# Products of attention values in 64x64 tiles of TensorE, for both sequences of a head group at once

## The chip, the cores and the metric

The kernel runs on one core of a Trainium2 chip. The metric is the device time of one execution in microseconds. Before the change it is 921.83 us, the median of three runs (920.75 to 923.23).

## The reference, cut to what matters

Sixteen sequences of 256 tokens of width 256 pass through two layers, each of the form x + s(xn) * silu(f(xn)) with xn the layer norm of x. In the first layer s is a linear recurrence and f a feed-forward block. In the second, s is causal attention with 16 heads and a key-value latent of 64, and f a linear layer with routed low-rank experts. Only the attention is touched:

```python
kv = x @ Wkv_a
c_kv, k_rope = (kv[..., :KV_LORA], kv[..., KV_LORA:])
c_kv = c_kv * rsqrt(mean(c_kv * c_kv) + RMS_EPS) * kv_norm_w
kv = (c_kv @ Wkv_b).reshape(B, S, N_HEADS, QK_NOPE + V_DIM)
scores = jnp.where(mask, einsum('bqhd,bkhd->bhqk', q, k) * scale, min)
attn = softmax(scores)
out = einsum('bhqk,bkhd->bqhd', attn, v).reshape(B, S, N_HEADS * V_DIM)
return out @ Wo
```

The kernel folds Wkv_b into the query weights and into Wo. So scores are taken against the 128 values of a key row (64 latent, 64 rotated), and the product of values multiplies the probabilities with the 64 latent values c_kv alone.

## The kernel before

All data are float32. The first 300 us are the first layer; behind it comes a loop (line 1603) over 64 units. A chunk is 512 tokens, that is two sequences (b = 0 and 1); its 16 heads form four groups g of G = 4 heads. A unit is one sequence of one group, so a group is two successive units and a chunk eight (r = 0 to 7). Helpers at the top record every operation in the order of the program for each engine (class InOrder); therefore nearly every instruction of the profile has line 53, and the reading goes by tile names.

For a unit, score_pack (line 1354) makes the scores in three packs, each in one PSUM bank of a ring of three (tile sc): block a of 32 queries of four heads stands in 128 partitions and meets the 32 (a + 1) keys that the causal mask leaves. VectorE (DVE) masks the diagonal and takes the maxima (nm); ScalarE (ACT) writes the exponentials to pr and their sums to sr; normalise (line 1386) takes reciprocals on DVE and scales pr on GpSimd (POOL).

The product needs the probabilities with keys in partitions. turn (line 1399) transposes 32x32 squares on DVE into the tile turned, in three thirds: queries 0 to 127 with keys 0 to 127, queries 128 to 255 with keys 0 to 127, and queries 128 to 255 with keys 128 to 255. send (line 1411) writes turned to DRAM (tile far, three buffers) with four DMAs, one for each head, and fetch (line 1423) brings it back as pT with one DMA, so that 128 keys stand in partitions; pT has three buffers. values (line 1442) then multiplies, for each pair of heads p2, each key block kb of 128 and each head hh of the pair: the stationary operand is the 64 latent values of 128 key rows (k.row), the moving operand pT, 256 columns for the first block and 128 for the second, and the output 64 partitions (half hh) of a PSUM bank av. ACT copies av to attT, which finish_mm or fast_mm multiply with the output weights. For the last two units turn_here (line 1427) transposes on PE instead of going through DRAM.

The order in the loop is written by hand. In unit i, SP first gets fetch of unit i - 2, later send of unit i - 1, and in even units query_move (line 419), eight DMAs that place rotated queries into qg. PE takes values of units i - 4 and i - 3 together in even i, between score packs 1 and 2 (units 0 and 1 at i = 4 and 5, the last ones behind the loop). All DMAs of SP stand in one queue and are issued one by one; an issue that waits holds those behind it.

The latent rows come about once per chunk: kv_begin (line 266) at r = 4 and kv_end (line 293) at r = 5 write k.row of the next chunk, with two buffers; key_chunk (line 299) at r = 7 transposes it to kT for the scores. The working tiles of PE's results (m1: av, pq and others) share a ring of five PSUM banks.

Of the kernel before, what the change touches and what calls it, by code (L numbers as in the profile page):

```python
# [11 lines left out]
F32 = mybir.dt.float32  # L12
# [6 lines left out]
P = 128  # L19
B, S, D = 16, 256, 256  # L20
NTOK = B * S
CH = 512
NCH = NTOK // CH
TPC = CH // P
# [5 lines left out]
NOPE, ROPE, VD, KVL = 128, 64, 128, 64  # L30
# [11 lines left out]
def tile_two_layers(ctx: ExitStack, tc: tile.TileContext, d: dict, out: bass.AP):  # L42
# [54 lines left out]
    pe = InOrder(nc.tensor)  # L97
# [103 lines left out]
    def bc(ap, n):  # L201

        return ap.unsqueeze(1).to_broadcast([ap.shape[0], n, ap.shape[1]])
# [8 lines left out]
    ak = ctx.enter_context(tc.tile_pool(name="ak1", bufs=2))  # L212
# [5 lines left out]
    sp = InOrder(nc.sync)  # L218
    ve = InOrder(nc.vector)
    ac = InOrder(nc.scalar)  # L220
# [3 lines left out]
    def m1(name, shape):  # L224
        return place["pool"].tile(shape, F32, tag=place["tag"], name=name)
# [4 lines left out]
    chunks = [Chunk() for _ in range(NCH)]  # L230
# [35 lines left out]
    def kv_begin(ch):  # L266

        k = chunks[ch]
        k.pkv = pkv = m1(f"pkv_{ch}", [P, TPC, P])
        for j in range(TPC):  # L270
            for c in range(2):
                pe.matmul(
                    pkv[:, j, :], k.xnT[:, c, j * P : (j + 1) * P], wkva[:, c, :],
                    start=(c == 0), stop=(c == 1),
                )
        k.row = ak.tile([P, TPC, P], F32, tag="row", name=f"row_{ch}")
        k.tmp = tmp = ak.tile([P, 3, TPC, KVL], F32, tag="tmp", name=f"tmp_{ch}", bufs=1)
        sq, ra, rb = tmp[:, 0], tmp[:, 1], tmp[:, 2]
        ss = sm1.tile([P, TPC], F32, tag="ss", name=f"ss_{ch}")
        k.rk = sm1.tile([P, TPC], F32, tag="rk", name=f"rk_{ch}")  # L280
        ac.activation(sq, pkv[:, :, 0:KVL], AF.Square)
        x1_ = pkv[:, :, KVL : KVL + HR]
        x2_ = pkv[:, :, KVL + HR : P]
        ve.tensor_tensor(ra[:, :, 0:HR], x1_, rope_k[:, 0], ALU.mult)
        ve.tensor_tensor(ra[:, :, HR:ROPE], x2_, rope_k[:, 0], ALU.mult)
        ve.tensor_tensor(rb[:, :, 0:HR], x2_, rope_k[:, 1], ALU.mult)
        ve.tensor_tensor(rb[:, :, HR:ROPE], x1_, rope_k[:, 2], ALU.mult)
        ve.tensor_reduce(ss, sq, AX.X, ALU.add)
        ve.tensor_scalar(ss, ss, 1.0 / KVL, RMS_EPS, ALU.mult, ALU.add)
        gp.tensor_tensor(k.rk, ss, mhalf, ALU.pow)  # L290
        gp.tensor_tensor(k.row[:, :, KVL:P], ra, rb, ALU.add)

    def kv_end(ch):
        k = chunks[ch]
        sq = k.tmp[:, 0]
        ve.tensor_tensor(sq, k.pkv[:, :, 0:KVL], bc_in(k.rk, KVL), ALU.mult)
        ve.tensor_tensor(k.row[:, :, 0:KVL], sq, bc(kvw_bc, TPC), ALU.mult)

    def key_chunk(ch):
        k = chunks[ch]  # L300
# [67 lines left out]
    G = 4  # L368
    NG = NH // G
# [59 lines left out]
    with ExitStack() as l0:  # L429
# [151 lines left out]
        u = tiny("u")  # L581
# [234 lines left out]
        def fast_weights1():  # L816
            w12 = x1.tile([P, 2, FH], F32, tag="xnT", name="w12")
            w56 = x1.tile([P, 2, FH], F32, tag="xn", name="w56", bufs=1)
            fw.w = {1: w12[:, 0], 2: w12[:, 1], 5: w56[:, 0], 6: w56[:, 1]}
            fw.w[7] = ak.tile([P, FH], F32, tag="kT", name="w7")  # L820
            g = g0
            g.tensor_tensor(fw.w[1], a1(0, 0), a1(1, 1), ALU.add)
            g.tensor_tensor(fw.w[5], a1(0, 0), a1(0, 1), ALU.add)
            g.tensor_tensor(fw.w[2], a1(1, 0), a1(1, 1), ALU.add)
            g.tensor_tensor(fw.w[6], a1(0, 0), a1(1, 0), ALU.subtract)
            g.tensor_tensor(fw.w[7], a1(1, 1), a1(0, 1), ALU.subtract)
            fw.w[3], fw.w[4] = a1(0, 0), a1(1, 1)
            x36 = ak.tile([P, 2, S], F32, tag="row", name="x36")
            x417 = ak.tile([P, 3, S], F32, tag="tmp", name="x417", bufs=1)
            fw.x = {3: x36[:, 0], 4: x417[:, 0], 1: x417[:, 1]}  # L830
            fw.x6 = [x36[:, 1], w0.tile([P, S], F32, tag="bst", name="x6")]
            fw.x7 = [x417[:, 2], w0.tile([P, S], F32, tag="bsc", name="x7")]
            misc = qr.tile([P, 2, CH], F32, tag="qrot", name="misc")
            fw.f = misc[:, 0, :].rearrange("p (i s) -> p i s", i=2)
            fw.db = misc[:, 1, 0:DH]

        def fast_weights2():
            t12 = x1.tile([P, 2, 4, DH], F32, tag="xnT", name="t12")
            fw.t = {1: t12[:, 0], 2: t12[:, 1]}
            fw.t[3] = ak.tile([P, 4, DH], F32, tag="row", name="t3")  # L840
            fw.t[4] = ak.tile([P, 4, DH], F32, tag="kT", name="t4")
            g = g0
            g.tensor_tensor(fw.t[1], b2(0, 1), b2(0, 0), ALU.subtract)
            g.tensor_tensor(fw.t[2], b2(1, 1), fw.t[1], ALU.subtract)
            g.tensor_tensor(fw.t[4], fw.t[2], b2(1, 0), ALU.subtract)
            g.tensor_tensor(fw.t[3], b2(1, 1), b2(0, 1), ALU.subtract)
            g.tensor_tensor(fw.db, b2_bc[:, DH:D], b2_bc[:, 0:DH], ALU.subtract)
# [562 lines left out]

    def send(u):

        u.far = dp.tile([4, 32, G, 3, P], F32, tag="far", name=f"far_{u.n}", bufs=3)
        for h in range(G):
            sp.dma_start(
                u.far[:, :, h, :, :].rearrange("k s z q -> s k z q"),
                u.turned[32 * h : 32 * h + 32, :, :, :],
            )

    def new_pT(u):  # L1420
        u.pT = pp.tile([P, G, 3, P], F32, tag="pT", name=f"pT_{u.n}", bufs=3)

    def fetch(u):
        new_pT(u)
        sp.dma_start(u.pT, u.far.rearrange("k s h z q -> (k s) h z q"))

    def turn_here(u, z):

        if z == 1:
            new_pT(u)  # L1430
        a0, k0 = THIRDS[z]
        pt = m1(f"pt_{u.n}_{z}", [P, CH])
        for y in range(4):
            o = OFF[a0] + y * WID[a0] + 32 * k0
            pe.transpose(pt[:, y * P : (y + 1) * P], u.pr[:, o : o + P], ident)
        for y, e in ((0, ac.copy), (2, ve.tensor_copy)):
            e(
                u.pT[:, :, z, 32 * y : 32 * y + 64].rearrange("p h (a q) -> p a h q", q=32),
                pt[:, y * P : (y + 2) * P].rearrange("p (a h q) -> p a h q", a=2, h=G),
            )  # L1440

    def values(u, e=None):
        k, b = chunks[u.ch], u.b
        av = m1(f"av_{u.n}", [P, 2, S])
        for p2 in range(2):
            for kb in range(2):
                for hh in range(2):
                    h = 2 * p2 + hh
                    pe.matmul(
                        av[64 * hh : 64 * hh + 64, p2, P * kb : S].rearrange(  # L1450
                            "p (z s) -> p z s", s=P
                        ),
                        k.row[:, 2 * b + kb, 0:KVL],
                        u.pT[:, h, 2:3, :] if kb else u.pT[:, h, 0:2, :],
                        start=(kb == 0), stop=(kb == 1),
                    )
        if b == 0:
            k.attT.append(a2.tile([P, 2, CH], F32, tag="attT", name=f"attT_{u.n}", bufs=6))
        (e or ac.copy)(k.attT[u.g][:, :, b * S : (b + 1) * S], av)

    def finish_mm(ch, j, p0, p1):
        k = chunks[ch]
        if p0 == 0:
            if ch == NCH - 1 and j < 3:
                k.po[j] = ps_sc.tile([P, CH], F32, tag="sc", name=f"po_{ch}_{j}")
            else:
                k.po[j] = m1(f"po_{ch}_{j}", [P, CH])
        for p in range(p0, p1):
            pe.matmul(
                k.po[j][:, 0:D], k.attT[p // 2][:, p % 2, j * P : (j + 1) * P], wout[:, p, :],  # L1470
                start=(p == 0), stop=(p == NPAIR - 1),
            )
# [130 lines left out]
    for i in range(LAST):  # L1603
# [7 lines left out]
        last = ch - 1 if ch == NCH - 1 and r in FINISH else None  # L1611
        fast = ch - 1 if 0 < ch < NCH - 1 else None

        if 2 <= i:
            fetch(units[i - 2])
        score_pack(u, 0)
        if w:
            normalise(w, (2,))
# [28 lines left out]
            if not odd:  # L1647
                query_lat(n, 3)
        if i == 5:
            values(units[1])  # L1650
        score_pack(u, 1)

        if odd and n is not None:
# [10 lines left out]
        if not odd:  # L1664
            if n is not None and i != 2:
                query_move(n)
            if i >= 4:
                values(units[i - 4])
            if i > 4:
                values(units[i - 3])  # L1670
        score_pack(u, 2)
        normalise(u, (0, 1))

# [25 lines left out]
    normalise(u1, (2,))  # L1699

    finish_mm(ch, 0, 0, 4)
    values(units[LAST - 4])
    finish_mm(ch, 1, 0, 4)
    turn_here(u1, 1)
    turn_here(u1, 2)
    values(units[LAST - 3], ve.tensor_copy)
    values(u0)
    turn_here(u1, 0)
    for j in range(TPC):
# [80 lines left out]
```

## Time and profile before

| what | value |
|---|---|
| median of the runs | 921.83 us |
| span of the profiled execution | 919.9 us, 1.9 less than that median |
| mean granted TensorE clock | 0.996 |
| PE, DVE, POOL, ACT busy | 905.2, 666.4, 570.6, 465.8 us |
| fetches pT<-far | 62 of 768 KB, 5.0 us from issue to landing |
| sends far<-turned | 248 of 192 KB, 4.3 us |
| moves qg<-qrot | 256 of 64 KB, 2.3 us |

The span runs from the first to the last instruction of one execution; what lies around it (start and end) is in the time and not in the span. "Busy" is time in which an engine has at least one instruction, so that two products which run at once count once; the mean duration of one record stands behind it. PEld is the loading of stationary operands, which runs beside the products. "a<-b" names the tile that is written and a tile that is read. The chain of work that ended last follows the execution back from its end, at each step to what released it; what is not on it did not set the end.

### The profile page before, as it was taken

How to read it: one execution, taken by the hardware profiler on the slowest of the kernel's cores; microseconds unless marked ns; L12 is line 12 of the kernel's file. 1: busy time of each engine (PE TensorE's matmuls, PEld its weight loads, DVE VectorE, ACT ScalarE, POOL GpSimd, SP SyncE). 2: the span in 40 equal slices, each digit the busy share in tenths (PEclk: the TensorE clock that was granted, in tenths of full speed). 3: DMA queues.
4: the chain of work that ended last, by engine and by line, in shares of the span. 5: the costliest groups of instructions: out<-in, count | busy, mean ns of one | idle time of the engine just before them, and what ended most of it. 6: DMA issues, size and time to landing. Idle time of an engine off the chain costs nothing.

```text
span 919.9 us, 17382 instructions
## 1 busy us (share of the span) xinstructions
PE 905.2 (98%) x5426; PEld 695.4 (76%) x5426; DVE 666.4 (72%) x2018; ACT 465.8 (51%) x1529; POOL 570.6 (62%) x885
## 2 busy tenths in 40 slices
PE   8999999999999899999999999999999999999998
PEld 7768898987767567777777777777777777777776
DVE  6876687664688779668967866896786689677562
ACT  3335555654336545645644564564466456446541
POOL 1228697777355537686586767648676764866541
PEclk9999999999999999999999999999999999999999
DMA  9730000000025777777776777777677777767771
GB/s 280 232 115 1 1 2 1 1 2 1 1 32 106 201 203 184 203 186 186 178 210 160 208 194 192 189 178 207 159 209 206 181 190 178 205 160 211 206 224 42
DMA packets 196412, 134.00 MB, mean 146 GB/s; under 512 B 142112, under 2 KB 186976, under 8 KB 196320
## 3 DMA queue, kind: packets, MB, share of 16 engines
q1 hardware_dynamic: 194192, 128.68, 53.3%
q0 software_dynamic: 1152, 3.67, 1.2%
q8 instruction: 44, 0.72, 0.3%
q10 hardware_dynamic: 976, 0.53, 0.2%
q14 instruction: 48, 0.39, 0.1%
HBM read 63.11 MB, written 52.95 MB: 126 GB/s over the span
## 4 chain that ended last, share of the span: by engine, by line
PE 90%; DVE 3%; DMA 2%; SPq 2%; POOL 1%; issue 1%; ACT 0%; POOLq 0%; DVEq 0%; ACTq 0%
PE pq L53 22%; PE sc L53 14%; PE po L53 10%; PE av L53 9%; PE r L53 7%; PE f L53 7%; PE ph L53 5%; PE pf L53 5%; PE pg L53 4%; PE pm L53 2%; SPq L53 2%; PE pkv L53 1%; PE tp L53 1%; DMA qg<-qrot 1%; PE py L53 1%; PE pb L53 1%
## 5 line engine op out<-in xcount | busy, mean ns | idle before, releaser
L53 ACT ACTIVATE pr<-sc,nm 128x256 f32<-128x256 f32 (+7 forms) x512 | 189.7, 381 | 240.3 <-DVE sr L53 152.2
L53 POOL TENSOR_SCALAR pr<-pr,sr 128x256 f32<-128x256 f32 (+7 forms) x512 | 192.1, 394 | 190.0 <-DVE sr L53 184.1
L53 PEld LDWEIGHTS sc<-kT,qg 128*128 128x128 f32 x1024 | 157.6, 191 | 62.3 <-issue 40.3
L53 PE MATMUL sc<-kT,qg 128*128 128x256 f32 (+7 forms) x1024 | 176.1, 306 | 5.7 <-DMA qg<-qrot 4.4
L53 DVE TENSOR_REDUCE nm<-sc 128x1 f32<-128x256 f32 (+7 forms) x512 | 127.5, 301 | 6.6
L53 DVE STREAM_TRANSPOSE turned<-pr 128x512 f32<-128x512 f32 x186 | 123.2, 687 | 9.6 <-POOL pr L53 8.7
L53 PE MATMUL pq<-xnT,wlat 128*128 128x512 f32 x256 | 124.1, 608 | 0.0
L53 PE MATMUL pq<-xnT,wrope 128*128 128x512 f32 x256 | 120.2, 593 | 0.0
L53 ACT ACTIVATION_READ_ACCUMULATOR pr<-sc,nm 128x1 f32 x512 | 104.3, 204 | 0.0
L53 DVE TENSOR_TENSOR sc<-sc,kmask 128x96 f32<-128x96 f32 (+1 forms) x192 | 45.5, 237 | 64.9 <-PE sc L53 63.9
L53 PE MATMUL av<-pT,row 128*64 128x256 f32 (+1 forms) x1024 | 90.9, 329 | 0.5 <-DMA pT<-far 0.5
L53 POOL TENSOR_TENSOR qrot<-qmul,qmul 128x512 f32<-128x512 f32 x64 | 83.0, 1317 | 8.0 <-POOL pr L53 2.9
L53 PEld LDWEIGHTS av<-pT,row 128*64 128x64 f32 x1024 | 64.1, 137 | 24.3 <-issue 1.6
L53 DVE TENSOR_TENSOR qmul<-pq,rot_q 128x512 f32<-128x512 f32 x128 | 80.7, 672 | 0.1
L53 ACT ACTIVATE qg<-pq 64x512 f32<-64x512 f32 x128 | 75.4, 589 | 5.4 <-PE pq L53 4.7
L53 PEld LDWEIGHTS pq<-xnT,wlat 128*128 128x128 f32 x256 | 46.0, 192 | 32.0 <-issue 32.0
L53 PEld LDWEIGHTS pq<-xnT,wrope 128*128 128x128 f32 x256 | 45.7, 191 | 32.4 <-issue 32.1
L53 PEld LDWEIGHTS po<-wout,attT 128*128 128x128 f32 x416 | 58.4, 191 | 9.5 <-issue 4.9
L53 PE MATMUL po<-wout,attT 128*128 128x128 f32 (+1 forms) x416 | 64.5, 308 | 0.0
L53 POOL TENSOR_TENSOR rs<-ve,mhalf 128x4 f32<-128x4 f32 (+1 forms) x17 | 16.8, 986 | 51.3 <-DVE ve L53 37.0
L53 PE MATMUL ph<-xnT,p1T 128*128 128x256 f32 (+1 forms) x128 | 44.3, 503 | 0.8 <-DVE xnT L53 0.8
L53 POOL TENSOR_TENSOR attT<-attT,attT 128x512 f32<-128x512 f32 x36 | 45.0, 1270 | 0.0
(226 smaller groups left out, 1505.0 us busy)
## 6 DMA issues: line engine op xcount, KB each, us to landing
far<-turned SPq DMA_DIRECT2D x248, 192.0 KB, 4.3
pT<-far SPq DMA_DIRECT2D x62, 768.0 KB, 5.0
qg<-qrot SPq DMA_DIRECT2D x256, 64.0 KB, 2.3
x<-in_x_dram SPq DMA_DIRECT2D x7, 512.0 KB, 9.3
out_dram<-x POOLq DMA_DIRECT2D x12, 256.0 KB, 4.9
wqn_wo<-in_wq_nopeT_dram SPq DMA_DIRECT2D x4, 512.0 KB, 4.9
wqn_wo<-in_Wo_dram SPq DMA_DIRECT2D x4, 512.0 KB, 6.1
p2T<-in_proj2T_dram SPq DMA_DIRECT2D x2, 512.0 KB, 7.2
```

What stands on the lines that cost most here:

```text
L53: r = getattr(self.engine, name)(*args, **kw)
```

## The change

The products of values of a group are made for both sequences together (values_of), with keys in blocks of 64. Partitions 0 to 63 of the operands hold sequence 0 and partitions 64 to 127 sequence 1; an output half hh and a sequence b together name one 64x64 tile of TensorE, and av has one PSUM bank for each sequence. The moving operand is that of two heads at once, with 512, 384, 256 and 128 columns for key blocks 0 to 3. The stationary operand comes from a new tile rowv, in which kv_end places the latent rows with four copies on ACT; k.row now has one buffer. far holds a whole group (two buffers), and fetch brings it in odd units with four DMAs of 64 partitions into one pT with a single buffer. values_of(n) stands in unit i = 2n + 4 (group 0 at i = 5); group 30 is behind the loop, and the last group is made as before, with its pT in the buffers of turned.

```diff
 def kv_end(ch):
...
+        if ch == 0:
+            rowv.append(ak.tile([P, 2, 4, KVL], F32, tag="rowv", name="rowv", bufs=1))
+        k.rowv = rowv[0][:, ch % 2]
+        for b in range(2):
+            for y in range(2):
+                ac.copy(
+                    k.rowv[64 * b : 64 * b + 64, y::2, :],
+                    k.row[64 * y : 64 * y + 64, 2 * b : 2 * b + 2, 0:KVL],
+                )
...
-        u.far = dp.tile([4, 32, G, 3, P], F32, tag="far", name=f"far_{u.n}", bufs=3)
+        q = groups[u.i // 2]
+        if u.b == 0:
+            q.far = dp.tile([2, 4, 32, G, 3, P], F32, tag="far", name=f"far_{u.n}", bufs=2)
...
-    def fetch(u):
-        new_pT(u)
-        sp.dma_start(u.pT, u.far.rearrange("k s h z q -> (k s) h z q"))
+    def fetch(n):
+
+        q = groups[n]
+        q.pT = pp.tile([P, 2, G, 3 * P], F32, tag="pT", name=f"pT_{n}", bufs=1)
+        far = q.far.rearrange("b (y k) s h z q -> y b (k s) (h z q)", y=2)
+        for y in range(2):
+            for b in range(2):
+                sp.dma_start(
+                    q.pT[64 * b : 64 * b + 64, y].rearrange("p h q -> p (h q)"), far[y, b]
+                )
...
+    def values_of(n):
+
+        q = groups[n]
+        ch, g = divmod(n, NG)
+        k = chunks[ch]
+        av = [m1(f"av_{ch}_{g}_{b}", [P, 2, S]) for b in range(2)]
+        for z, c0 in enumerate((0, 64, S, S + 64)):
+            n0 = 64 * z
+            heads = q.pT[:, z % 2, :, c0 : c0 + S - n0].rearrange("p (a hh) q -> p a hh q", hh=2)
+            for b in range(2):
+                rows = slice(64 * b, 64 * b + 64)
+                for hh in range(2):
+                    pe.matmul(
+                        av[b][64 * hh : 64 * hh + 64, :, n0:S], k.rowv[rows, z, :],
+                        heads[rows, :, hh, :], start=(z == 0), stop=(z == 3),
+                    )
+        k.attT.append(a2.tile([P, 2, CH], F32, tag="attT", name=f"attT_{ch}_{g}", bufs=6))
+        for b in range(2):
+            ac.copy(k.attT[g][:, :, b * S : (b + 1) * S], av[b])
...
-        if 2 <= i:
-            fetch(units[i - 2])
+        if odd and i > 2:
+            fetch((i - 3) // 2)
...
         if i == 5:
-            values(units[1])
+            values_of(0)
...
-            if i >= 4:
-                values(units[i - 4])
             if i > 4:
-                values(units[i - 3])
+                values_of((i - 4) // 2)
...
     finish_mm(ch, 0, 0, 4)
-    values(units[LAST - 4])
     finish_mm(ch, 1, 0, 4)
+    values_of(LAST // 2 - 2)
     turn_here(u1, 1)
     turn_here(u1, 2)
-    values(units[LAST - 3], ve.tensor_copy)
     values(u0)
```

More of the change, by code (lines that the diff above doesn't have):

```diff
@@ L275, in kv_begin @@
                 )
-        k.row = ak.tile([P, TPC, P], F32, tag="row", name=f"row_{ch}")
+        k.row = ak.tile([P, TPC, P], F32, tag="row", name=f"row_{ch}", bufs=1)
         k.tmp = tmp = ak.tile([P, 3, TPC, KVL], F32, tag="tmp", name=f"tmp_{ch}", bufs=1)
@@ L291, in kv_begin @@
         gp.tensor_tensor(k.row[:, :, KVL:P], ra, rb, ALU.add)
+    rowv = []
     def kv_end(ch):
@@ L827, in fast_weights1 @@
             fw.w[3], fw.w[4] = a1(0, 0), a1(1, 1)
-            x36 = ak.tile([P, 2, S], F32, tag="row", name="x36")
+            x36 = ak.tile([P, 2, S], F32, tag="row", name="x36", bufs=1)
             x417 = ak.tile([P, 3, S], F32, tag="tmp", name="x417", bufs=1)
@@ L839, in fast_weights2 @@
             fw.t = {1: t12[:, 0], 2: t12[:, 1]}
-            fw.t[3] = ak.tile([P, 4, DH], F32, tag="row", name="t3")
+            fw.t[3] = ak.tile([P, 4, DH], F32, tag="rowv", name="t3", bufs=1)
             fw.t[4] = ak.tile([P, 4, DH], F32, tag="kT", name="t4")
@@ L1411, in send @@
     def send(u):
-        u.far = dp.tile([4, 32, G, 3, P], F32, tag="far", name=f"far_{u.n}", bufs=3)
+        q = groups[u.i // 2]
+        if u.b == 0:
+            q.far = dp.tile([2, 4, 32, G, 3, P], F32, tag="far", name=f"far_{u.n}", bufs=2)
         for h in range(G):
             sp.dma_start(
-                u.far[:, :, h, :, :].rearrange("k s z q -> s k z q"),
+                q.far[u.b, :, :, h, :, :].rearrange("k s z q -> s k z q"),
                 u.turned[32 * h : 32 * h + 32, :, :, :],
@@ L1420, in new_pT @@
     def new_pT(u):
-        u.pT = pp.tile([P, G, 3, P], F32, tag="pT", name=f"pT_{u.n}", bufs=3)
-    def fetch(u):
-        new_pT(u)
-        sp.dma_start(u.pT, u.far.rearrange("k s h z q -> (k s) h z q"))
+        u.pT = pp.tile([P, G, 3, P], F32, tag="turned", name=f"pT_{u.n}", bufs=2)
+    def fetch(n):
[7 more added lines that the diff above has]
+                )
     def turn_here(u, z):
```

## The prediction

> **What bounds the kernel now.** I read the page's busy shares first, then the chain of work that ended last, the groups of PE split by shape, and the timeline of one stretch in the middle with PE and SP side by side.
>
> ```profile
> span 919.9 us, 17382 instructions
> PE 905.2 (98%) x5426; PEld 695.4 (76%) x5426; DVE 666.4 (72%) x2018; ACT 465.8 (51%) x1529; POOL 570.6 (62%) x885
> PE 90%; DVE 3%; DMA 2%; SPq 2%; POOL 1%; issue 1%; ACT 0%; POOLq 0%; DVEq 0%; ACTq 0%
> PE pq L53 22%; PE sc L53 14%; PE po L53 10%; PE av L53 9%; PE r L53 7%; PE f L53 7%; PE ph L53 5%; PE pf L53 5%; PE pg L53 4%; PE pm L53 2%; SPq L53 2%; PE pkv L53 1%; PE tp L53 1%; DMA qg<-qrot 1%; PE py L53 1%; PE pb L53 1%
> ```
>
> PE is busy 98% of the span and is 90% of the chain; the products of values (tile av) are 9% of the chain by themselves, some 83 us. From 340 to 860 us the window view shows PE at 19.4 to 20.0 of every 20 us. So a microsecond less of PE work there is a microsecond less of time, as long as nobody else becomes late.
>
> ```profile
> L53 PE MATMUL pq<-xnT,wlat 128*128 128x512 f32 x256 | 124.1, 608 | 0.0
> L53 PE MATMUL av<-pT,row 128*64 128x256 f32 x512 | 78.8, 386 | 0.5 <-DMA pT<-far 0.5
> L53 PE MATMUL av<-pT,row 128*64 128x128 f32 x512 | 49.8, 273 | 0.0
> L53 PE MATMUL pg<-wbase,xnT 128*128 128x256 f32 x128 | 33.5, 384 | 0.0
> L53 PE MATMUL py<-csc,hs 64*128 64x256 f32 x64 | 9.1, 401 | 0.0
> ```
>
> The program has 512 products of values and the trace 1024 records: each float32 product is two passes. Busy time over count is 262 ns for a full 128x128 pass of 256 columns (pg), but 154 for av and 142 for py. The av products stand in two column halves (heads hh 0 and 1), py in two row halves (sequences b 0 and 1): in both, two run at once.
>
> ```profile
> 488.14 2.82 PE L53 MATMUL av<-pT,row 128*64 128x256 f32 x32
> 489.98 2.19 SPq L53 DMA_DIRECT2D far<-turned  x4
> 492.27 6.10 SPq L53 DMA_DIRECT2D qg<-qrot  x8
> 498.48 0.56 SPq L53 DMA_DIRECT2D pT<-far  x1
> 503.76 1.80 SPq L53 DMA_DIRECT2D far<-turned  x4
> 507.07 2.82 PE L53 MATMUL av<-pT,row 128*64 128x256 f32 x32
> 509.42 0.34 SPq L53 DMA_DIRECT2D pT<-far  x1
> ```
>
> One period (two units) is some 19.5 us: on PE one block of 32 av passes, on SP a fetch in each unit, four sends in each and eight moves of rotated queries. The block that begins at 507.07 needs the fetch of 498.48, issued 8.6 us before. The starts of the records show 2.75 us from a block's first pass to the pass behind it.
>
> **Part 1: passes on PE.** Before, each unit issues, per half of the columns, 2 x (256 + 128) columns in two passes. The records stand in pairs: two starts 7 ns apart, then 216 ns to the next pair at 256 columns and 109 at 128. Two units are 16 pairs: 8 x 216 + 8 x 109 = 2.60 us; the other 0.15 us of the 2.75 lies at the block's ends. After, a group issues four products for each of four key blocks, of 512, 384, 256 and 128 columns, again 32 passes. Each tile then streams 1280 columns twice instead of 1536, because a finer key block drops more of the causal half. A 512-column pass is 430 ns (four pq records last 1.72 us on the chain), 384 lies between at 323. If four tiles run at once: 2 x (430 + 323 + 216 + 109) = 2.16, three more starts at 7 ns 0.02, the same ends 0.15: 2.33 us. That is 0.42 less for each of 29 groups, 12.2 us. Groups 0 and 30 stood as two single blocks of 1.45, 2.90, and save 0.57 each. The last group stays as it was. Sum **-13.3 us**.
>
> That four run at once is not in this trace: it shows columns split in two and rows split in two, each at full rate, never both. Bounds from the nearest rows: four at once (2.33), or only two (2 x 2.16 + 0.15 = 4.46). I take four: py's two row halves write all 128 partitions of two PSUM banks, as av[0] and av[1] will, and av's two halves already read two streams from each row.
>
> Against this stands a rule. In py and in av the last pair both end products, and the first two starts are 7 ns apart: the second product's first pass does not wait for the first product's second. The Trainium skill, "TensorE: Matmul & The Clock Gate", Part 3, The mechanism, says that matmuls start and end strictly in program order; with two passes of a product in succession this would let only two tiles overlap and make a block 4.46 us. The pairs speak against that reading. The Trainium skill, "TensorEngine Tiling (Array Packing)", When to Use Tiling recommends row tiling where the contraction is at most 64; here it was 128, so by that rule the tiles bring nothing. The working agrees: all of the 0.42 us comes from columns that the finer blocks leave out (1280 against 1536).
>
> **Part 2: copies of rows.** kv_end gets four ACT copies of 64x128 in each of 8 chunks. The nearest row is the copy of 128x128 (bT<-psb), 265 ns: 32 x 0.27 = 8.5 us on ACT, which is busy 51%. They lie at r = 5. There a bank of scores is free again 8 to 9 us before its next products start (the exps' ends against the starts of the score packs three packs on), so they are covered: 0. Without that cover, 1.1 us per chunk. That av's two copies now come together delays one by about 0.9 us; five m1 banks cover it.
>
> **Part 3: transfers.** Each group's fetch is now four DMAs of 384 KB, all in the odd unit, where two of 768 KB stood in two units; bytes are the same. SP issues two more per group, at 0.34 to 0.56 us, but none in the even unit. There a fetch now lies ahead of sends and moves: the first three moves at 533.54 take 0.78, 0.93 and 1.12 us where the others take 0.63. Without it the moves and the odd fetch should come about 1 us earlier. The odd fetch also waits for the block before, through the single pT buffer; that block ended 7 us or more before every odd fetch, so this hides.
>
> The landing is what can hurt. 768 KB take 5.0 us, and the packets of a running fetch move some 310 KB per us, so the second 768 KB land 2.5 us later, at 7.5. The first two DMAs hold the keys of z = 0, the other two those of z = 1, wanted 0.86 us into the block. Lead needed: 6.6 us. The leads of the four groups of a chunk are about 10.8, 8.6, 6.3 and 5.6: two are short, by 0.3 and 1.0, and gain about 1 from the earlier fetch. I take 0; if SP gains nothing it is 1.3 us in each of some 7.5 chunks, 10 us. The sends behind the fetch land later, but they have two units.
>
> **Part 4: both ends.** At 321.68 PE stands 3.47 us behind moves that SP issued late, with the fetch of the unit before ahead of them. This fetch goes; between 0 and -3.5, I take **-1.5**. At the end PE has less work between transfers: the block at 885.24 already waited for its fetch (issued 879.45, landed 885.10). Its second half now lands 2.5 us later, and values_of(30) stands ahead of the last transposes; between 0 and +4, I take **+2.0**.
>
> **Sum:** -13.3 - 1.5 + 2.0 = -12.8, a span of 907.1. The median of the runs is 921.83, 1.9 above the span, so 909.0 us.
>
> **Rivals.**
> - *Two tiles at a time* (slower): each block is 4.46, +1.71 x 31 = +53 us, about 975. For it: no record of four. Against: the pairs. It decides at once, since the gain is gone when a block exceeds 2.75. Chance 0.09.
> - *Staggered*: the second row half starts one pass late, as its products come behind those of the first in order. Each block is 430 ns longer, 2.76, the gain is nil: with the ends 922. Chance 0.08.
> - *The fetch lands late* (slower): all bytes of a group in one burst, into one buffer. At 2 us late in the two short phases, 15 blocks x 2 = 30: -12.8 + 30, about 939. It passes no gain once stalls average 0.43 us per group. For it: leads of 5.6 and 6.3. Against: the free even unit, and packets of sends begin only as those of the fetch end. Chance 0.12, a quarter of it still faster.
> - *Absorbed*: DVE is busy 18.7 of 20 us between 600 and 620; a faster PE meets it there. Half the gain, about 916. Chance 0.04.
>
> **Numbers.** The forecast has 0.67; its own range, from the bounds of part 4 and some absorption, is 904 to 916. The range takes in the staggered case and the mild late fetches: 903 to 926. About 0.3% is what a measurement here can tell from no change. Faster: the forecast 0.67, absorbed 0.03, late 0.03, together 0.73. Same: staggered 0.07, late 0.02, absorbed 0.01, together 0.10. Slower: two at a time 0.09, late 0.07, staggered 0.01, together 0.17.
>
> **What would show it.** Right: av blocks of 2.3 us with four starts within some 25 ns, no PE wait for pT<-far in the middle, moves of 0.63 us each. Wrong: pairs instead of fours in the block, or 2.7 us and more (rivals one and two); PE waiting for pT<-far inside blocks at two phases of each chunk (three); scores waiting for DVE or ACT where PE had no gap (four).

## The result, and the profile after

The changed kernel takes 946.26 us (median of four runs, 941.63 to 956.51) beside 922.53 for the kernel before: a ratio of **1.024 [1.0211 to 1.0268]**, where the prediction had 909.0. The run at 956.51 lies more than 1.5% above the fastest of the four and is left out of the ratio. The profiled run took 946.94 us, of which the span is 945.2. From the page of the changed kernel: the busy line, the granted clock by slice, the chain of work that ended last, the two groups of the products of values, and the DMA issues (KB each, median us from issue to landing).

```profile
span 945.2 us, 17425 instructions
...
PE 921.8 (98%) x5426; PEld 684.8 (72%) x5426; DVE 665.3 (70%) x2017; ACT 477.9 (51%) x1562; POOL 571.6 (60%) x885
...
PEclk9999999999999899999989999999999999999979
...
PE 68%; DMA 13%; SPq 7%; DVE 6%; POOL 5%; issue 1%; ACT 1%; DVEq 0%; POOLq 0%; ACTq 0%
PE pq L53 13%; DMA pT<-far 12%; PE sc L53 9%; PE po L53 8%; SPq L53 7%; PE r L53 7%; PE f L53 7%; PE av L53 6%; PE ph L53 5%; PE pf L53 4%; PE pg L53 3%; POOL pr L53 2%; PE pkv L53 2%; PE pm L53 1%; PE tp L53 1%
...
L53 PE MATMUL av<-pT,rowv 64*64 64x512 f32 (+2 forms) x992 | 98.7, 451 | 14.1 <-DMA pT<-far 13.9
...
L53 PEld LDWEIGHTS av<-pT,rowv 64*64 64x64 f32 x992 | 44.8, 135 | 64.6 <-DMA pT<-far 36.6
...
far<-turned SPq DMA_DIRECT2D x248, 192.0 KB, 4.0
pT<-far SPq DMA_DIRECT2D x124, 384.0 KB, 5.9
```

PE is busy 98% as before, which tells nothing: a matmul that stands waiting inside a block is partly counted as busy (of some 38 us of waits, counted below, only 14.1 stand as idle time of PE). The chain tells it. PE fell from 90% of the chain to 68%, and the fetch pT<-far, which the chain of before did not list at all, is now 12%, some 113 us, with SP's queue another 7%. The wait stands at the weight load (36.6 us on PEld), since that is the first instruction of a product.

The timeline of the changed kernel shows a block that found its data and the next one, which did not (columns: start, us, engine, instruction, count, idle time before and its releaser).

```profile
580.12 2.38 PE L53 MATMUL av<-pT,rowv 64*64 64x512 f32 x32
...
591.47 2.49 SPq L53 DMA_DIRECT2D pT<-far  x4
...
598.61 0.21 PEld L53 LDWEIGHTS av<-pT,rowv 64*64 64x64 f32 x8
598.61 1.85 PE L53 MATMUL av<-pT,rowv 64*64 64x512 f32 x12
...
599.60 0.20 PEld L53 LDWEIGHTS av<-pT,rowv 64*64 64x64 f32 x4 [0.78 <-DMA pT<-far]
...
601.21 1.27 PEld L53 LDWEIGHTS av<-pT,rowv 64*64 64x64 f32 x20 [1.41 <-DMA pT<-far]
601.21 1.51 PE L53 MATMUL av<-pT,rowv 64*64 64x384 f32 x20 [0.74 <-DMA pT<-far]
```

The block at 598.61 begins 7.14 us after its fetch was issued. It stops before its second set of products and again at 601.21, 9.74 us after the issue, when the last DMA has landed.

Laid over all blocks (from a block's first pass to the pass behind it), the PE time of the products of values grew from 89.07 to 113.14 us, **+24.1 of the span's +25.3**. A block without a wait takes 2.31 us where it took 2.75. What stands above 2.31 adds up to 38.6 us: 10.1 in the blocks of groups 1 and 29, near the two ends, and 28.5 in the other 29. (Some 2.6 us of the 10.1 are not waits but passes at half clock, as the section on the prediction shows.) So the products did get faster by the amount forecast, and waits for the fetch took back nearly three times that.

By the group's place in a chunk (medians of the blocks of groups 4 to 27, us from the first of the fetch's DMAs; the lead is the time to the block's start, and half has landed when the first two of the four DMAs have):

```
place   lead    half landed   last landed   wait in the block
0       6.85       6.19          9.66            1.86
1      14.39       6.29          9.62            0.00
2       8.19       6.37          9.73            1.03
3       7.52       6.20          9.58            1.33
```

A block waits where its lead is shorter than the last landing by more than about 0.9 us, the time it spends on its first half: 9.66 - 6.85 - 0.86 is 1.95, and 1.86 was measured. It is the last landing that ends the wait: of the 23 blocks that wait, 19 end 1.49 us behind it, to the hundredth.

### The profile page after: what moved, and what is told of

Read it like the earlier page. It is cut to its first block, busy times and chain, and to the rows that moved or that the text cites. A ratio compares the mean times of both kernels' runs of the same rounds, so it can differ in the third digit from the quotient of the medians.

```text
span 945.2 us, 17425 instructions
## 1 busy us (share of the span) xinstructions
PE 921.8 (98%) x5426; PEld 684.8 (72%) x5426; DVE 665.3 (70%) x2017; ACT 477.9 (51%) x1562; POOL 571.6 (60%) x885
## 4 chain that ended last, share of the span: by engine, by line
PE 68%; DMA 13%; SPq 7%; DVE 6%; POOL 5%; issue 1%; ACT 1%; DVEq 0%; POOLq 0%; ACTq 0%
PE pq L53 13%; DMA pT<-far 12%; PE sc L53 9%; PE po L53 8%; SPq L53 7%; PE r L53 7%; PE f L53 7%; PE av L53 6%; PE ph L53 5%; PE pf L53 4%; PE pg L53 3%; POOL pr L53 2%; PE pkv L53 2%; PE pm L53 1%; PE tp L53 1%
## 5 line engine op out<-in xcount | busy, mean ns | idle before, releaser
L53 PEld LDWEIGHTS sc<-kT,qg 128*128 128x128 f32 x1024 | 159.6, 193 | 57.2 <-issue 42.7
L53 PE MATMUL sc<-kT,qg 128*128 128x256 f32 (+7 forms) x1024 | 178.2, 309 | 1.3 <-ACT pr L53 1.3
L53 PE MATMUL av<-pT,rowv 64*64 64x512 f32 (+2 forms) x992 | 98.7, 451 | 14.1 <-DMA pT<-far 13.9
L53 PEld LDWEIGHTS av<-pT,rowv 64*64 64x64 f32 x992 | 44.8, 135 | 64.6 <-DMA pT<-far 36.6
L53 PEld LDWEIGHTS po<-wout,attT 128*128 128x128 f32 x416 | 60.7, 198 | 10.0 <-issue 5.0
L53 PE MATMUL po<-wout,attT 128*128 128x128 f32 (+1 forms) x416 | 66.8, 316 | 0.0
L53 POOL TENSOR_TENSOR rs<-ve,mhalf 128x4 f32<-128x4 f32 (+1 forms) x17 | 16.8, 988 | 52.4 <-DVE ve L53 38.5
```

The costliest lines, as they stand in the source:

```text
L53: r = getattr(self.engine, name)(*args, **kw)
```

## Experiments

All times are medians with the ratio to the kernel before, run on the same chip, and its 95% interval.

**Theory.** The block is as fast as forecast, and the time goes into waits for a fetch that lands 2 us later than worked out, because its DMAs write 64 partitions each. **Rivals:** the four tiles themselves are slower or disturb the engines around them; or the burst of a whole group is to blame, whatever the form of its DMAs; or SP, with more DMAs to issue, is late.

**1. No fetch but the first (e2).** All later groups use the probabilities of group 0.

```diff
 def fetch(n):
     q = groups[n]
+    if n:
+        q.pT = groups[0].pT
+        return
```

> Edit: only group 0 is fetched; groups 1 to 30 multiply group 0's probabilities, so 120 of the 124 fetch DMAs (46 MB) are left out; the products themselves are all made. Theory that the fetch alone costs the time: all blocks of values 2.31 us, time 921.8 - 13.3 minus what SP and the queues gain at the start, 903 to 910. Rival (the products in 64x64 tiles, the copies of rows or the two copies of av that now come together hold PE up as well): blocks over 2.5 us in the mean, or time over 915.

903.64 us, **0.9809 [0.9794, 0.9823]**. The page of this run, and the window from 540 to 640 us (length, busy us and count of each engine, granted clock, DMA share, GB/s):

```profile
span 902.8 us, 17264 instructions
...
PE 91%; DVE 4%; POOL 1%; DMA 1%; ACT 1%; SPq 1%; issue 1%; DVEq 0%; ACTq 0%; POOLq 0%
```

```profile
540.00:640.00 100.00, 100.00 (x650) 74.05 (x643) 74.68 (x237) 54.50 (x211) 73.14 (x122) 1.00 0.52 111
```

The same window of the changed kernel:

```profile
540.00:640.00 100.00, 97.68 (x590) 69.03 (x588) 72.39 (x229) 54.90 (x207) 65.72 (x114) 1.00 0.78 181
```

In these 100 us PE runs 650 matmuls where the changed kernel runs 590, at the same clock. A window holds other parts of the work in each kernel; from 340 to 840 us it is 3191 against 3017. All 31 blocks take 2.31 us.

From here on a chunk is timed from its first product of tile pg to the next chunk's, which gives seven times, and the tail is what follows the last of these products. The last whole chunks take 78.95 us where before they took 80.68: 1.73 less, four times 0.43. (The three chunks ahead of them gain 0.9 to 1.7 us; there PE waits up to 1.05 us before one score product.) So neither the tiles nor DVE, ACT or the copies of rows cost anything once the loop runs evenly; nearly all of the loss hangs on the fetches. Of the 42.3 us between this span and the changed kernel's, 38.5 stand as waits in blocks.

**2. The same fetch, wanted later (e3).** values_of moves from behind the second score pack of an even unit to that unit's end.

```diff
         if not odd:
             if n is not None and i != 2:
                 query_move(n)
-            if i > 4:
-                values_of((i - 4) // 2)
...
+        if not odd and i > 4:
+            values_of((i - 4) // 2)
```

> Edit: values_of stands at the end of the even unit instead of ahead of score pack 2; nothing else. This gives the same fetch 3 to 5 us more. Theory (fetch lands late): of the waits of 38.6 us in the blocks at most 8 stay, time 908 to 922. Rival (waits of the blocks are of another kind, or the fetch is held back by the block before through the single buffer): a block that comes later leaves the waits as they are, time 938 to 950.

910.56 us, **0.9885 [0.9869, 0.9901]**. The landing is unchanged at 9.6 to 9.7 us; the leads are 8.96, 14.87, 11.60 and 8.95. The page:

```profile
span 909.3 us, 17418 instructions
...
PE 93%; DVE 3%; DMA 1%; POOL 1%; ACT 1%; SPq 1%; issue 0%; POOLq 0%; ACTq 0%
```

DMA is back to 1% of the chain, and whole chunks behind the first take 78.94 to 79.7 us. Waits in blocks fall from 38.6 to 7.6 us, of which 5.2 stand in one block, that of group 29 near the end:

```profile
867.65 1.07 PE L53 MATMUL av<-pT,rowv 64*64 64x512 f32 x4
...
869.41 1.08 PE L53 MATMUL av<-pT,rowv 64*64 64x512 f32 x4 [0.69 <-DMA pT<-far]
...
871.41 0.86 PE L53 MATMUL av<-pT,rowv 64*64 64x384 f32 x4 [0.92 <-DMA pT<-far]
...
872.81 2.37 PE L53 MATMUL av<-pT,rowv 64*64 64x384 f32 x20 [0.54 <-DMA pT<-far]
```

There PE reaches its block soon after the fetch was issued and takes the four DMAs one by one as they land. The same burst of the same DMAs, only with 1.4 to 3.4 us more lead at the three short places, turns +2.4% into -1.15%.

**3. The form of the fetch, in the kernel before (e4, e6).** Each fetch of 768 KB is split into two DMAs: by partitions (e4, two times 64), or by heads (e6, each over all 128). Nothing else differs from before.

```diff
-        sp.dma_start(u.pT, u.far.rearrange("k s h z q -> (k s) h z q"))
+        far = u.far.rearrange("k s h z q -> (k s) h z q")
+        for y in range(2):
+            sp.dma_start(u.pT[64 * y : 64 * y + 64], far[64 * y : 64 * y + 64])   # e4
+            sp.dma_start(u.pT[:, 2 * y : 2 * y + 2], far[:, 2 * y : 2 * y + 2])   # e6
```

> Edit on the kernel before the change: each fetch of 768 KB is split into two DMAs of 64 partitions each (384 KB); everything else as before. Rate theory: packets of 6144 bytes go from 234 ns in the median to 400 or more and the second half lands 6.5 us or more after the first issue (before: 5.0); since the leads there are 5.6 us and more, the time rises only to 922 to 930. If the slower packets of the changed kernel come from another thing (its layout in DRAM, the traffic of a whole group at once), the packets stay at about 234 ns and the time at 921 to 923.

> Control to e4, on the kernel before the change: each fetch again as two DMAs of 384 KB, but split by heads (3 KB of each of 128 partitions) instead of by partitions. If the partitions are the cause in e4: packets of 3072 bytes take 117 to 130 ns in the median (the rate of 6144 in 234), time 921 to 925. If two DMAs in place of one are the cause: over 180 ns, and the time of e4, 926.

e4 took 926.49 us, **1.0059 [1.0044, 1.0074]**; e6 took 916.38, **0.994 [0.9925, 0.9955]**. Their DMA issues, e4 first:

```profile
pT<-far SPq DMA_DIRECT2D x124, 384.0 KB, 5.0
```

```profile
pT<-far SPq DMA_DIRECT2D x124, 384.0 KB, 3.8
```

Before, 768 KB in one DMA landed in 5.0 us; over 64 partitions half of that takes as long. The packet records say the same: 6144 B in 234 ns (median) before, 418 ns in e4 and 436 ns in the changed kernel, and 3072 B in 121 ns in e6. The two DMAs of e4 together landed 5.93 us after the first issue, those of e6 5.15. So at two DMAs each, the 64 partitions cost 0.8 us of landing. Both split fetches leave the chunks in the middle at 80.68 us, since the kernel before has leads to spare; they differ at the ends. The first chunk takes 72.7 us in e4, 69.0 in e6 and 71.2 before; the tail 90.1, 84.1 and 86.7. That e6 is faster than the kernel before was not expected, and its cause stays open: all 768 KB land no sooner than the 5.0 us of before, and the gain lies in the first chunk and the tail.

**4. The form of the fetch, in the changed kernel (e1, e9).** A fetch over 128 partitions needs far in another order, and each send must then be split in two. So e1 does both, and e9 splits the sends alone.

```diff
 for h in range(G):
-    sp.dma_start(q.far[u.b, :, :, h, ...], u.turned[32 * h : 32 * h + 32])
+    for y in range(2):                                    # e1 and e9
+        sp.dma_start(..., u.turned[32 * h : 32 * h + 32, 2 * y : 2 * y + 2])
...
 for y in range(2):
-    for b in range(2):
-        sp.dma_start(q.pT[64 * b : 64 * b + 64, y], far[y, b])
+    sp.dma_start(q.pT[:, y], far[y])                      # e1 only
```

> Edit: far is laid out so that the two sequences of one half y lie one behind the other; a group is fetched by two DMAs over all 128 partitions (768 KB each) instead of four over 64 partitions. To write this layout each send is split in two, eight more of 96 KB per unit pair and head group. Rate theory (a DMA that writes only 64 partitions runs slower): the 6144-byte packets, 436 ns in the median in the changed kernel, come back to about 234 as before; the second half lands some 7.5 us after the first issue instead of about 10; the waits inside the blocks of values fall from 38.6 us to 15 or less and the time to 915 to 930. Burst theory (the bytes come too late because a whole group is fetched in one unit, whatever the rate): packets may get faster, but the time stays over 935. Third theory (the waits in the blocks are not the transfer's): blocks as long as now, 940 to 950.

> Control to e1, on the changed kernel: each send is split in two by halves y (eight more of 96 KB per group), while layout and fetch stay as they are (four DMAs of 64 partitions). It tells what the extra sends cost in e1, and so what the faster packets alone gave there. If the extra sends cost nothing: waits in the blocks as in the changed kernel, 38 us, time 940 to 948, and the whole of e1's gain is the packets'. If they shorten the leads (e1's leads of 5.7 to 7.1 us stand against 6.9 to 8.2): 948 to 962, and the packets gave more than e1 shows.

e1 took 935.13 us, **1.0159 [1.0126, 1.0192]**, e9 989.58, **1.0744 [1.0703, 1.0785]**. Issues and landings, e1 first:

```profile
far<-turned SPq DMA_DIRECT2D x496, 96.0 KB, 2.7
pT<-far SPq DMA_DIRECT2D x62, 768.0 KB, 5.7
```

```profile
far<-turned SPq DMA_DIRECT2D x496, 96.0 KB, 2.8
pT<-far SPq DMA_DIRECT2D x124, 384.0 KB, 6.4
```

At equal sends the form of the fetch is worth 54 us; by an estimate, up to some 26 us of that are the clock, which ran at half speed for 58.0 us of e9 and for some 5 us of e1 (behind the first 20). In e1 the packets are back at 234 ns, half the group has landed at 4.91 us and all of it at 7.64, where e9 has 6.3 and 9.7. These are the 5.0 and 7.5 of the prediction. But eight more sends per group cost SP time: e9 alone is 43 us slower than the changed kernel, its leads at places 0 and 2 fall to 5.74 and 6.76, and e1's to 5.97 and 7.09. So e1 still waits 24.1 us in blocks (e9: 56.9). That lies between the theories written down for e1: the packets came back as the rate theory said, but neither the waits (15 or less) nor the time (915 to 930) did. The price of the sends was under-estimated in the expectation for e9, which had 948 to 962. SP's waits name what it stands for in e9 from 437 to 843 us, a wait of which the changed kernel has 0.6 us there (why SP waits for the fetch was not followed further):

```profile
SPq L53 <- DMA pT<-far: 53.1, 43, 1.8
```

**5. Key blocks in the order in which they land (e7).** The first two DMAs hold key blocks 0 and 2, the others 1 and 3.

```diff
-        for z, c0 in enumerate((0, 64, S, S + 64)):
+        for z, c0 in ((0, 0), (2, S), (1, 64), (3, S + 64)):
```

> Edit on the changed kernel: the four key blocks are taken in the order 0, 2, 1, 3, so that both blocks of the first half (0 and 2) stand ahead of those of the second. The second half is then wanted 1.29 instead of 0.86 us into the block. Theory (the last landing ends the wait): 0.43 us less in each of some 23 waiting groups, waits 38.6 to about 29 us, time 934 to 940. Rival (waits of another kind): 944 to 948.

943.6 us, **1.0237 [1.022, 1.0255]**: no measurable gain in the median, and the expected 934 to 940 were missed. The waits in blocks fall from 38.6 to 32.5 us, but they are read from the fastest of its four runs (939.57; the others took 943 to 944). More work now stands ahead of the wait, but the leads changed too (7.12 at place 0, but 6.70 at place 3), as the whole pipeline moves with the waits.

**6. Half of the fetch a unit earlier (e5).** Sequence 0 in the even unit, sequence 1 in the odd one; the tile still has one buffer.

```diff
-        if odd and i > 2:
-            fetch((i - 3) // 2)
+        if 2 <= i:
+            fetch(units[i - 2])      # two DMAs, of sequence b alone
```

> Edit on the changed kernel: the fetch is split again over the two units, sequence 0 in the even unit and sequence 1 in the odd one, two DMAs of 64 partitions in each; the single buffer stays, so the even fetch waits for the block of values of the same unit. Rate theory alone (64 partitions are slow, spreading does not matter): waits in the blocks stay above 25 us, time over 935. Burst theory (what is late is the second 768 KB of one unit): the odd fetch lands in some 6 us as in e4, leads are 6.9, 14, 8.2 and 7.5 us, so the waits in the middle are under 3 us in all; the even fetch holds SP up behind the block, which costs 0 to 5 us at the start and in the phase with the longest lead: 906 to 918.

939.15 us, **1.0178 [1.0135, 1.0221]**: the expectation failed. The waits in blocks did go (8.4 us left, mostly at the ends), but the time did not. The even fetch now overwrites the tile that the block of the same unit reads, and it stands at the head of SP's queue. SP's waits of e5 from 437 to 843 us, and then, over the whole span, PE's waits of score products for moved queries (us in total, times, longest):

```profile
SPq L53 <- DMA far<-turned: 89.7, 51, 5.0
SPq L53 <- PE av L53: 15.0, 5, 3.8
```

```profile
PE sc L53 <- DMA qg<-qrot: 12.4, 5, 7.5
```

The timeline shows it once in full: a block runs from 555.50 to 558.13, the even fetch is issued at 558.38, the sends at 559.51, and the moves of rotated queries only at 562.74. The kernel before has SP waiting for far<-turned too (72.5 us in its middle), but 0.3 us for av. The first chunk takes 78.55 us instead of 72.0, the others 79.9 to 82.0, and the tail 93.1; in the kernel before these are 71.2, some 80.7 and 86.7. So e5 loses most at both ends, where all but 2.2 us of the waits for moved queries lie (before has 4.4 in all), and 13.6 us at half clock between 320 and 352 add to the first chunk. How much is the late moves, how much the burst of sends behind the fetch and how much the clock was not separated.

**7. Later, wide and reordered together (e8).**

> Edit: e3 (block at the end of the even unit), e1 (fetch over 128 partitions, sends split in two) and the order 0, 2, 1, 3 together. Theory: leads of 9 us and more against a landing of 7.6, no waits in the middle, the last one at the end of the kernel (5.2 us in e3) shortened by 2 to 2.5: 906 to 909, 2 to 4 under e3. If eight more sends for each group hold SP up so that other things become late: 910 or more.

916.1 us, **0.9936 [0.992, 0.9952]**, with the edits of e1, e3 and e7. Waits in blocks are nearly gone (1.5 us), yet it is slower than e3 and misses 906 to 909: its first chunk takes 68.35 us where e3's takes 64.1. Once the lead covers the slow landing, a faster landing brings little. That the extra sends are the cost is likely, but no run has e8 without them.

**8. Later, and the ends mended (e10).** e3, with the block of group 29 moved behind the output products of the last unit, and that of group 30 behind the products of unit 62.

```diff
-        if not odd and i > 4:
+        if not odd and 4 < i < LAST - 2:
             values_of((i - 4) // 2)
...
+            values_of(LAST // 2 - 3)      # in the last unit, behind its output products
...
-    values_of(LAST // 2 - 2)
     turn_here(u1, 1)
     turn_here(u1, 2)
     values(u0)
+    values_of(LAST // 2 - 2)
```

> Edit on e3: group 29's block moves behind the output products at the head of the last unit, and group 30's block behind the product of unit 62 and the last transposes. e3 waits 5.2 us in group 29's block, while everything from the last chunk's first gate to the end takes 92.7 us there against 83.0 with no fetch at all (e2). Theory (the end is short of lead as the middle was): the 5.2 us go, 904 to 907. If group 30's fetch, which waits for group 29's block, becomes late in its place: 908 to 912.

907.7 us, **0.9839 [0.9821, 0.9857]**: the fastest of the kernels that compute all of it.

```profile
span 906.5 us, 17418 instructions
...
PE 90%; DVE 3%; DMA 2%; POOL 2%; ACT 1%; issue 1%; SPq 1%; POOLq 0%; ACTq 0%
```

The tail falls from 92.7 us (e3) to 88.5, and 4.3 us of waits in blocks are left; the time lies just above the 904 to 907 expected. Two whole buffers for pT, which would take the wait off e5's fetch, were not tried.

## Why the prediction was wrong

**Part 1, passes on PE: right.** 2.33 us per block were forecast and 2.31 measured. The records begin at 580.120, .127, .133 and .140, and the next four at 580.600: four tiles run at once, each first pass beside the others. Over all blocks the gain without waits is 13.7 us (89.07, less the 0.74 us that one block of before waited, to 74.64 in e2), against 13.3. One term was misread: group 30 stood as one block of 1.45 us and half of a block of 2.75 that it shared with unit 62, so it saved 0.43 and not 0.57 (the last two groups went from 5.65 to 5.22 us). The rivals "two at a time" (4.46 us per block) and "staggered" (2.76) are out.

**Part 2, copies: right.** In e2 they are all there, in every chunk; no block is longer than its passes make it, and neither are the last three whole chunks.

**Part 3, transfers: the step that failed.** It put the waits at 0, or at 10 us if SP gained nothing. It said: "the packets of a running fetch move some 310 KB per us, so the second 768 KB land 2.5 us later, at 7.5." That rate was read from DMAs over 128 partitions and carried to DMAs over 64. Measured, the second half came 3.4 us after the first (226 KB per us), at 9.65, and the first half at 6.25 instead of 5.0. With it the "lead needed" of 6.6 us became 8.8, and three places of four fell short of it instead of two by 0.3 and 1.0. The leads themselves came near the forecast: at the two shortest places about 1 us more than the 6.3 and 5.6 of before (7.52 and 6.85), so the odd fetch did move forward and SP was not late; at the third 8.19 for 8.6, and at the longest 14.39 for 10.8. e1 shows that the working was sound for 128 partitions (4.91 and 7.64), and e4 that the 64 partitions are what slows the packets, without any of the tiles.

The trace of before showed no fetch over 64 partitions, so the rate was an unseen cost, and it should have been bounded from both sides: at half the 310 KB per us the second half lands 5 us after the first, at 10 us or later. With the landing as measured, the prediction's own leads (10.8, 8.6, and 6.3 and 5.6 with 1 us gained) give waits of 0, 0.2, 1.5 and 2.2 us, 3.9 in each of 7.5 chunks, 29 us: more than twice the gain, and a slower kernel.

The Trainium skill, "SBUF — State Buffer", section Door 1: The DMA port swizzle, says that 64 partitions in a row reach only 8 of the 16 ports, and gives 196 GB/s for them beside 328 for all 128, at 1 MiB. The same page, under "Can I just issue two DMAs to hit both halves?", says that two such DMAs do not add up. The runs here agree in direction, with a smaller gap: 226 KB per us in the changed kernel beside 281 in e1 (768 KB in 2.73 us), and 5.93 us for e4's pair beside 5.15 for e6's and 5.0 for the one DMA of the same bytes.

**Part 4, the ends: wrong in size.** The end was put at +2.0, between 0 and +4. The tail grew by 7.0 us (86.7 to 93.7), and the block of group 29 alone waits 5.8. It is the same step: that block starts 4.4 us behind its fetch, so it pays most of the later landing. Against e2's tail of 83.0 it is 10.7 us; besides the 5.8, the 10.2 us at half clock that begin there (below) can by an estimate make up to 3.8 of it. The start was put at -1.5; the first chunk came at 72.0 against 71.2, while e2, without later fetches, has 66.3, and e3, with them, 64.1. So the gain there was larger than thought, and waits and clock took it.

**The rival that came true** is "the fetch lands late", put at 939 us with a chance of 0.12. Its mechanism and its place are those of the trace. Its price of 30 us came out as 28.5 in the middle, partly by luck: it had two places at 2 us, and there were three at 1.0 to 1.9. The 10.1 at the ends it did not count. The clock adds to it: 23.9 us of the changed kernel's span after the start ran at half the granted clock (6.8 at 325.8, 6.8 at 472.5, 10.2 at 906.0), against 3.4 before. The windows around the second show it (the clock is the third number from the end):

```profile
465.00:470.00 5.00, 4.44 (x23) 2.41 (x23) 3.90 (x11) 3.12 (x12) 4.22 (x7) 1.00 1.00 227
470.00:475.00 5.00, 4.28 (x33) 3.05 (x30) 0.47 (x3) 1.48 (x5) 2.43 (x2) 0.75 1.05 339
475.00:480.00 5.00, 5.00 (x28) 5.00 (x27) 1.76 (x10) 1.38 (x7) 2.05 (x6) 0.56 0.68 100
```

PE has gaps in the first two windows and is then busy all the time at about half speed. The chunk around it took 87.16 us, 3.0 more than the 78.95 of e2 and its own 5.2 us of waits make. The other two stretches begin inside the blocks of groups 1 and 29, which end 2.80 us behind their last landing instead of 1.49. That the waits bring the low clock is likely, as e2 has none of it after the start, but no run tried it by itself, and the two do not go in step: e5, with 8.4 us of waits in blocks, has 13.6 us of it.

"Absorbed" is out: in e2 PE is busy 100.00 of 100 us.

## What to carry to other kernels

A faster block on the bounding engine earns its time only if its inputs come sooner by as much; so set the lead of each block against the landing of its last DMA, place by place, and price the landing for the partitions that each DMA writes. Splitting an operand by partition halves to suit a row-tiled product made its fetch about half as fast per packet, and a group of 1.5 MB landed at 9.65 us where it landed at 7.64 over all 128. Where the lead is short, moving the consumer later by a fraction of a stage can be worth more than mending the transfer: it took 36 us here without touching a DMA, where the wide fetch with its extra sends took 11.

## What the runs showed of the hardware

- Two DMAs of 384 KB over 128 partitions, with rows of 3 KB, landed in 3.8 us each, and the second 5.15 us after the first was issued, where one of 768 KB with rows of 6 KB took 5.0. The kernel before became 0.6% faster with this as the only edit (e6); why is open.
- Issuing a 384 KB DMA over 64 partitions took SP 594 ns (581 in e4), and one of 768 KB over 128 partitions 338 ns before: the smaller one was dearer to issue. One of 384 KB over 128 partitions took 338 ns too (e6).
- Splitting 248 sends of 192 KB into 496 of 96 KB cost 43 us in a kernel that stood on the landing of its fetches (e9). Its clock was at half speed for 58.0 us after the first 20, against 23.9, which by an estimate from these lengths makes up to 17 us of the 37 by which the span grew; the waits in blocks make another 18.
- Four 64x64 tiles of float32 products start 7 ns apart, and the block of 32 passes takes 2.31 us, what the eight passes of one tile were reckoned to take alone (2.33).
